# Graph attention with two residual layers on one core: written order on every engine, x kept on chip, q made on all partitions by one product

## The chip, the cores and the metric

The kernel runs on one core of a Trainium2 chip. The metric is the device time of one execution in microseconds (us). The kernel is written in Python against an engine-level language: every call names its engine (`nc.tensor` is TensorE, `nc.vector` VectorE, `nc.scalar` ScalarE, `nc.gpsimd` GpSimd, `nc.sync` the queue that issues most transfers), and a tile framework adds the semaphores. A pool with `bufs=n` gives n buffers to each tag; a tile that finds all of them in use waits until the oldest is free.

## The reference

Inputs are x (32 batches, 512 x 1024, float32), an adjacency matrix adj (512 x 512), two vectors wq and wk of 512, and biases. Only these steps are computed:

```python
# layer 0, per batch; C = 512, N = 1024
q = einsum('c,bcn->bn', wq, x)
k = einsum('c,bcn->bn', wk, x)
scores = q[:, None, :] + k[:, :, None]
scores = where(scores > 0, scores, 0.01 * scores)
att = softmax(scores, axis=-1)
agg = einsum('bcn,bmn->bcm', x, att)
x = layernorm(x + relu(einsum('oc,bcm->bom', adj, agg) + bm[None, :, None]))
# layer 1
W = adj * adj
x = layernorm(x + einsum('bnf,nm->bmf', x, W) + bias)
```

The 1024 x 1024 attention matrix is never made. Leaky ReLU splits each row of scores at q > -k, and on both sides exp(q + k) factors into a part of q and a part of k. So the kernel sorts the columns of z = adj x by q, forms running sums from both ends with the two weights, and each output column needs one row of either sum, found by counting how many q exceed -k.

## The kernel before

A batch goes through these functions. Names of tiles are those of the profile (z_ps, zbuf, sorted_z, up, zs, table, got, agg_ps, t, w, l_ps, g).

```python
xp = ctx.enter_context(tc.tile_pool(name="xp", bufs=2))
gp = ctx.enter_context(tc.tile_pool(name="gp", bufs=2))
# p2: 3 PSUM tiles of two banks, p1: 2 PSUM tiles of one bank

def scores(b):
    # ... t4 = four partial (q, k) pairs on TensorE, copied to qk4 by ScalarE
    for h in range(NH):
        nc.tensor.matmul(t2[0:2, h * H : (h + 1) * H], pick, qk4[:, h * H : (h + 1) * H], start=True, stop=True)
    nc.scalar.copy(rows, t2[0:2, :])
    for h in range(NH):        # q on all partitions
        nc.tensor.matmul(tq[:, h * H : (h + 1) * H], ones_row, rows[0:1, h * H : (h + 1) * H], start=True, stop=True)
    for j in range(NT):        # q and k as columns
        nc.tensor.transpose(tk[:, j, :], rows[:, j * P : (j + 1) * P], ident[0:2, 0:2])
    # ... qb = tq with its maximum (VectorE); eight ranks (VectorE), eight Sign counts (ScalarE)

def product(b, s):             # z = x^T adj^T, rows scattered to their ranks
    for j in range(NT):
        for c in range(CT):
            nc.tensor.matmul(t, xt[:, c, j * P : (j + 1) * P], adj_t[:, c, :], start=(c == 0), stop=(c == CT - 1))
        z = zbuf[j % ZB]       # ZB = 4
        nc.scalar.copy(z[:, 0:C], t)
        nc.gpsimd.tensor_copy(z[:, D : D + 1], s["qk"][:, j, 0:1])
        nc.gpsimd.indirect_dma_start(out=zd[:, :], ..., in_=z[:, :])

def sums(b, s):                # load sorted z, running sums up and down, carries, table
    nc.sync.dma_start(out=zs, in_=zd.rearrange("(p j) c -> p j c", j=NT))
    # ... ac: two exponents (ScalarE); 8 steps up into `up`, 8 steps down in zs (VectorE)
    # ... carries across partitions: TensorE, copied by ScalarE
    # ... carry added to `up`, written as the left half of each table row in three DMAs,
    #     then to zs, written as the right half in two

def mixed(b, s):               # one table row per output column
    for i in range(NT // G):   # G = 4
        for j in range(G):
            nc.gpsimd.indirect_dma_start(out=g[:, j, :], out_offset=None, in_=tb[:, :], ...)
        # ... weights w (VectorE), then per j: right half scaled (ScalarE), left half added (VectorE)

def layer0(b, parts):
    for o in range(CT):
        t = tp.tile([P, N], F32, tag="t", name=f"t_{b}_{o}")
        nc.sync.dma_start(out=t, in_=x[b, o * P : (o + 1) * P, :])
        # ... 8 transposes of parts into ps; t = max(ps, -bm) + t; mean, squares; then w2 = adj_2 / deviation

def layer1(b, ts, ws):
    # ... 32 products of 128 x 128 by 512 into ps; g = ps + bias; mean, squares
    for m, g in enumerate(gs):
        nc.vector.tensor_scalar(g, g, nmean[:, m : m + 1], rs[:, m : m + 1], ALU.add, ALU.mult)
        nc.sync.dma_start(out=out[b, m * P : (m + 1) * P, :], in_=g)

for i in range(B + 2):
    # load(i + 1), product(i), mixed(i - 1), scores(i + 1), layer1(i - 2), sums(i), layer0(i - 1)
```

This order is only a priority: the framework's scheduler may move an instruction ahead of another one on the same engine.

Of the kernel before, what the change touches and what calls it, by code (L numbers as in the profile page):

```python
# [26 lines left out]
BF16 = mybir.dt.bfloat16  # L27
U32 = mybir.dt.uint32
# [11 lines left out]
def adj_resnorm_kernel(  # L40
# [20 lines left out]
    xp = ctx.enter_context(tc.tile_pool(name="xp", bufs=2))  # L61
    one = ctx.enter_context(tc.tile_pool(name="one", bufs=1))
    gp = ctx.enter_context(tc.tile_pool(name="gp", bufs=2))
    tp = ctx.enter_context(tc.tile_pool(name="tp", bufs=CT + 1))
    op = ctx.enter_context(tc.tile_pool(name="op", bufs=CT))
    wp = ctx.enter_context(tc.tile_pool(name="wp", bufs=CT))
    sp = ctx.enter_context(tc.tile_pool(name="sp", bufs=2))
    dr = ctx.enter_context(tc.tile_pool(name="dr", bufs=1, space=bass.MemoryType.DRAM))
    p2 = ctx.enter_context(tc.tile_pool(name="p2", bufs=3, space=bass.MemoryType.PSUM))
    p1 = ctx.enter_context(tc.tile_pool(name="p1", bufs=2, space=bass.MemoryType.PSUM))  # L70

    def load(b):
        t = xp.tile([P, CT, N], F32, tag="x", name=f"x_{b}")
        for c in range(CT):
            nc.sync.dma_start(out=t[:, c, :], in_=x[b, c * P : (c + 1) * P, :])
        return t

    xts = {0: load(0)}


    ident = const.tile([P, P], F32, name="ident")
    make_identity(nc, ident)
    ones_row = const.tile([1, P], F32, name="ones_row")
    nc.vector.memset(ones_row, 1.0)
# [23 lines left out]
    wqk = const.tile([P, CT, 32], F32, name="wqk")  # L108
    nc.vector.memset(wqk, 0.0)
    nc.scalar.dma_start(out=wqk[:, :, 0:1], in_=wq.rearrange("(t p o) -> p t o", p=P, o=1))  # L110
    nc.scalar.dma_start(out=wqk[:, :, 1:2], in_=wk.rearrange("(t p o) -> p t o", p=P, o=1))
# [7 lines left out]
    nbm = const.tile([P, CT], F32, name="nbm")  # L119
    nc.scalar.dma_start(out=nbm, in_=bm.rearrange("(t p) -> p t", p=P))  # L120
    nc.vector.tensor_scalar(nbm, nbm, -1.0, None, ALU.mult)
    bias_b = const.tile([P, N], F32, name="bias_b")
    nc.scalar.dma_start(out=bias_b, in_=bias.partition_broadcast(P))

    adj_t = const.tile([P, CT, C], F32, name="adj_t")
    adj_2 = const.tile([P, CT, C], F32, name="adj_2")
    for r in range(CT):
        a = tp.tile([P, C], F32, tag="t", name=f"adj_{r}")
        nc.scalar.dma_start(out=a, in_=adj[r * P : (r + 1) * P, :])
        nc.vector.tensor_tensor(adj_2[:, r, :], a, a, ALU.mult)  # L130
        nc.vector.tensor_tensor(
            adj_2[:, r, r * P : (r + 1) * P], adj_2[:, r, r * P : (r + 1) * P], ident, ALU.add
        )
        t = p1.tile([P, CT, P], F32, tag="m", name=f"adj_tp_{r}")
        for c in range(CT):
            nc.tensor.transpose(t[:, c, :], a[:, c * P : (c + 1) * P], ident)
        nc.vector.tensor_copy(adj_t[:, :, r * P : (r + 1) * P], t)


    ZB = 4  # L140
    zbuf = [const.tile([P, ZR], F32, name=f"zbuf_{i}") for i in range(ZB)]
    for t in zbuf:
        nc.vector.memset(t[:, C : C + 1], 1.0)
    zero = const.tile([1, D], F32, name="zero")
# [3 lines left out]
    for t in table:  # L148
        nc.scalar.dma_start(out=t[N : N + 1, D:], in_=zero)

# [6 lines left out]
    def scores(b):  # L157
        xt = xts[b]
# [7 lines left out]
        qk4 = one.tile([P, N], F32, tag="qk4", name=f"qk4_{b}")  # L166
        for h in range(NH):
            nc.scalar.copy(qk4[:, h * H : (h + 1) * H], t4[:, h * H : (h + 1) * H])  # L168
        t2 = p2.tile([P, N], F32, tag="w", name=f"row_ps_{b}")
        for h in range(NH):  # L170
            nc.tensor.matmul(  # L171
                t2[0:2, h * H : (h + 1) * H], pick, qk4[:, h * H : (h + 1) * H],
                start=True, stop=True,
            )
        rows = one.tile([2, N], F32, tag="rows", name=f"rows_{b}")
        nc.scalar.copy(rows, t2[0:2, :])
        tq = p2.tile([P, N], F32, tag="w", name=f"q_ps_{b}")
        for h in range(NH):
            nc.tensor.matmul(
                tq[:, h * H : (h + 1) * H], ones_row, rows[0:1, h * H : (h + 1) * H],  # L180
                start=True, stop=True,
            )
        tk = p1.tile([P, NT, 2], F32, tag="m", name=f"col_ps_{b}")
        for j in range(NT):
            nc.tensor.transpose(tk[:, j, :], rows[:, j * P : (j + 1) * P], ident[0:2, 0:2])
        qb = one.tile([P, N], F32, tag="qb", name=f"qb_{b}")
        top = sp.tile([P, 1], F32, tag="top", name=f"top_{b}")
        nc.vector.tensor_scalar(qb, tq, 1.0, None, ALU.mult, ALU.max, accum_out=top)
        qk = sp.tile([P, NT, 2], F32, tag="qk", name=f"qk_{b}")
        nc.vector.tensor_copy(qk, tk)  # L190
        ntop = sp.tile([P, 2], F32, tag="ntop", name=f"ntop_{b}")
        nc.vector.tensor_scalar(ntop[:, 0:1], top, -1.0, None, ALU.mult)
        nc.vector.tensor_scalar(ntop[:, 1:2], top, -SLOPE, None, ALU.mult)

        rank = sp.tile([P, NT], F32, tag="rank", name=f"rank_{b}")
        sign = sp.tile([P, NT], F32, tag="sign", name=f"sign_{b}")
        for j in range(NT):
            junk = one.tile([P, N], BF16, tag="junk_v", name=f"junk_v_{b}_{j}")
            at = N - P - j * P
            nc.vector.scalar_tensor_tensor(  # L200
                junk, qb, qk[:, j, 0:1], tie[:, at : at + N], ALU.subtract, ALU.is_gt,
                accum_out=rank[:, j : j + 1],
            )
        for j in range(NT):
            junk = one.tile([P, N], BF16, tag="junk_s", name=f"junk_s_{b}_{j}")
            nc.scalar.activation(  # L206
                junk, qb, AF.Sign, bias=qk[:, j, 1:2], accum_out=sign[:, j : j + 1]
            )
        to = sp.tile([P, NT], U32, tag="to", name=f"to_{b}")
        nc.vector.tensor_copy(to, rank)  # L210
        of = sp.tile([P, NT], U32, tag="of", name=f"of_{b}")
        nc.vector.tensor_scalar(of, sign, 0.5, N / 2, ALU.mult, ALU.add)

        bd = sp.tile([P, 2, NT], F32, tag="bd", name=f"bd_{b}")
        nc.vector.tensor_scalar(bd[:, 0, :], qk[:, :, 1], top, 0.0, ALU.add, ALU.min)
        nc.vector.tensor_scalar(bd[:, 1, :], qk[:, :, 1], top, 0.0, ALU.add, ALU.max)
        nc.scalar.activation(bd[:, 0, :], bd[:, 0, :], AF.Exp, scale=1.0 - SLOPE)
        nc.scalar.activation(bd[:, 1, :], bd[:, 1, :], AF.Exp, scale=SLOPE - 1.0)
        return dict(qk=qk, ntop=ntop, to=to, of=of, bd=bd)

    def product(b, s):

        xt, zd = xts.pop(b), sorted_z[b % 2]
        ins = []
        for j in range(NT):
            t = p1.tile([P, C], F32, tag="m", name=f"z_ps_{b}_{j}")
            for c in range(CT):
                nc.tensor.matmul(  # L228
                    t, xt[:, c, j * P : (j + 1) * P], adj_t[:, c, :],
                    start=(c == 0), stop=(c == CT - 1),  # L230
                )
            z = zbuf[j % ZB]
            nc.scalar.copy(z[:, 0:C], t)  # L233
            nc.gpsimd.tensor_copy(z[:, D : D + 1], s["qk"][:, j, 0:1])  # L234
            ins.append(
                nc.gpsimd.indirect_dma_start(  # L236
                    out=zd[:, :], out_offset=bass.IndirectOffsetOnAxis(ap=s["to"][:, j : j + 1], axis=0),
                    in_=z[:, :], in_offset=None,
                ).ins
            )  # L240
        apart(f"ranks {b}", ins)

    def sums(b, s):

        zd, tb = sorted_z[b % 2], table[b % 2]
        zs = one.tile([P, NT, ZR], F32, tag="zs", name=f"zs_{b}")
        nc.sync.dma_start(out=zs, in_=zd.rearrange("(p j) c -> p j c", j=NT))
        ac = sp.tile([P, 2, NT], F32, tag="ac", name=f"ac_{b}")
        nc.scalar.activation(ac[:, 0, :], zs[:, :, D], AF.Exp, bias=s["ntop"][:, 0:1])
        nc.scalar.activation(ac[:, 1, :], zs[:, :, D], AF.Exp, scale=SLOPE, bias=s["ntop"][:, 1:2])  # L250
        up = one.tile([P, NT, D], F32, tag="up", name=f"up_{b}")
        nc.vector.tensor_scalar(up[:, 0, :], zs[:, 0, 0:D], ac[:, 0, 0:1], None, ALU.mult)
        for j in range(1, NT):
            nc.vector.scalar_tensor_tensor(  # L254
                up[:, j, :], zs[:, j, 0:D], ac[:, 0, j : j + 1], up[:, j - 1, :], ALU.mult, ALU.add
            )
        L = NT - 1
# [133 lines left out]
    for i in range(B + 2):  # L391
        if i + 1 < B:
            xts[i + 1] = load(i + 1)
# [41 lines left out]
```

## Time and profile before

| what | value |
|---|---|
| median of 3 runs | 3123.7 us (3109.84 to 3128.26) |
| profiled run | 3110.03 us, span 3108.3 us |
| busy: TensorE / VectorE / ScalarE / GpSimd | 2406.7 / 1710.3 / 1151.9 / 639.2 us |
| mean granted TensorE clock | 0.87 of full |
| moved by DMA | 608.14 MB, mean 196 GB/s |
| DMA queues, share of 16 engines | SyncE's 43.3%, GpSimd's 19.7% |

The page of the profile gives the busy time of each engine and the same in 40 equal slices. Its group lines name line, engine, operation, output and inputs, shape and count, then busy time and mean of one, then the idle time just before and what ended it. L228 is the product, L236 the scatter, L303 the gather, L200 the ranks, L206 the counts, L254 and L260 the sums up and down, L284, L286 and L292 the table's writes, L373 layer 1, L378 its output, L386 its normalization. "PEld" is the loading of a matmul's stationary operand, "SPq" the queue of SyncE. One float32 product of the source shows as two matmul instructions.

### The profile page before, as it was taken

The page shows a single profiled execution, that of the slowest core. Times are in us where ns is not written, and L with a number is a line of the kernel's source. Part 1 is how long each engine was busy: PE and PEld are TensorE (multiplying, and loading weights), DVE is VectorE, ACT ScalarE, POOL GpSimd, SP SyncE. Part 2 cuts the span into 40 slices and gives each one's busy share as a digit, 9 for nine tenths or more (in the row PEclk, how much of TensorE's full clock was granted, in tenths as well). Part 3 has the DMA queues.
Part 4 walks back from the last instruction along what each step waited for, and adds up shares of the span by engine and source line. Part 5 has one row for each costly group of instructions (what it writes and reads, how often), then busy time and mean ns, then how long its engine had stood idle before and what let it go on. Part 6 is the DMA issues. An engine that isn't in the chain of part 4 may idle for free.

```text
span 3108.3 us, 21737 instructions
## 1 busy us (share of the span) xinstructions
PE 2406.7 (77%) x6416; PEld 1050.7 (34%) x6416; DVE 1710.3 (55%) x3230; ACT 1151.9 (37%) x1982; POOL 639.2 (21%) x777
## 2 busy tenths in 40 slices
PE   6559877878778878778777778787777787788857
PEld 2224332333333334333333333343333343333423
DVE  4356654456645566644566445666445665445653
ACT  3134433334434344433344333344333444333422
POOL 2220222211222211222202222112222111222110
PEclk8779988989888889889898888898898988888968
DMA  5655656766566756567665577665677665685563
GB/s 190 190 152 160 222 196 192 244 164 199 202 190 220 221 177 204 201 186 230 195 177 203 184 217 238 162 204 200 192 222 206 187 200 199 188 239 177 162 203 129
DMA packets 187835, 608.14 MB, mean 196 GB/s; under 512 B 19106, under 2 KB 19106, under 8 KB 183620
## 3 DMA queue, kind: packets, MB, share of 16 engines
q1 hardware_dynamic: 128064, 403.28, 43.3%
q0 software_dynamic: 57344, 201.88, 19.7%
q10 hardware_dynamic: 2308, 1.58, 0.2%
q8 instruction: 51, 0.84, 0.1%
q14 instruction: 68, 0.56, 0.1%
HBM read 337.65 MB, written 269.03 MB: 195 GB/s over the span
## 4 chain that ended last, share of the span: by engine, by line
issue 30%; DVE 22%; PE 17%; DMA 16%; POOL 13%; ACT 2%; POOLq 0%; DVEq 0%; ACTq 0%
DMA got<-table,of 11%; DVE junk_v L200 7%; POOL got L303 6%; PE l_ps L373 6%; PE z_ps L228 5%; POOL sorted_z L236 5%; DMA sorted_z<-zbuf,to 4%; DVE g L378 3%; DVE up L254 3%; DVE got L318 3%; PE agg_ps L348 2%; PE row_ps L171 2%; POOL zbuf L234 2%; DVE zs L260 2%; ACT zbuf L233 1%
## 5 line engine op out<-in xcount | busy, mean ns | idle before, releaser
L373 PE MATMUL l_ps<-t,w 128*128 128x512 f32 x2048 | 1023.3, 663 | 247.9 <-DVE g L378 222.2
L228 PE MATMUL z_ps<-adj_t,x 128*128 128x512 f32 x2048 | 920.4, 600 | 47.4 <-ACT zbuf L233 47.4
L373 PEld LDWEIGHTS l_ps<-t,w 128*128 128x128 f32 x2048 | 432.9, 215 | 813.4 <-issue 546.6
L309 DVE TENSOR_TENSOR w<-bd,got 128x4 f32<-128x4 f32 x64 | 10.7, 167 | 1163.7 <-DMA got<-table,of 963.8
L228 PEld LDWEIGHTS z_ps<-adj_t,x 128*128 128x128 f32 x2048 | 380.1, 192 | 498.6 <-issue 418.1
L236 POOL DMA_INDIRECT sorted_z<-zbuf,to x256 | 276.7, 1081 | 1259.0 <-DVE g L386 1028.1
L233 ACT COPY zbuf<-z_ps 128x512 f32<-128x512 f32 x256 | 149.2, 583 | 859.0 <-DMA sorted_z<-zbuf,to 523.7
L200 DVE SCALAR_TENSOR_TENSOR junk_v<-qb,qk,tie 128x1024 bf16<-128x1024 f32 x256 | 327.4, 1279 | 0.4 <-DVE w L310 0.2
L317 ACT ACTIVATE got<-got,w 128x512 f32<-128x512 f32 x256 | 163.8, 711 | 428.1 <-DVE w L315 175.5
L234 POOL COPY zbuf<-qk 128x1 f32<-128x1 f32 x256 | 116.8, 478 | 998.8 <-DMA sorted_z<-zbuf,to 805.5
L206 ACT ACTIVATE junk_s<-qb,qk 128x1024 bf16<-128x1024 f32 x256 | 292.1, 1141 | 75.1 <-DVE qk L190 72.0
L171 PE MATMUL row_ps<-qk,pick 128*2 128x512 f32 x128 | 106.7, 982 | 267.5 <-ACT qk L168 267.5
L327 ACT ACTIVATE junk<-g,nmean 128x1024 bf16<-128x1024 f32 x128 | 147.0, 1149 | 364.7 <-DVE nmean L381 364.7
L303 POOL DMA_INDIRECT got<-table,of x256 | 242.8, 949 | 143.0 <-issue 69.8
L318 DVE SCALAR_TENSOR_TENSOR got<-got,w 128x512 f32<-128x512 f32 x256 | 175.3, 746 | 27.2 <-issue 15.8
L378 DVE SCALAR_TENSOR_TENSOR g<-l_ps,bias_b 128x1024 f32<-128x1024 f32 x128 | 155.9, 1218 | 35.1 <-PE l_ps L373 34.8
L254 DVE SCALAR_TENSOR_TENSOR up<-zs,ac,up 128x513 f32<-128x513 f32 x224 | 168.5, 752 | 4.4
L327 ACT ACTIVATE junk<-t,nmean 128x1024 bf16<-128x1024 f32 x128 | 146.6, 1145 | 64.1 <-DVE nmean L352 63.0
L260 DVE SCALAR_TENSOR_TENSOR zs<-zs,ac 128x513 f32<-128x513 f32 x224 | 167.4, 747 | 3.8
L348 PE MATMUL agg_ps<-ident,got 128*128 128x128 f32 x1024 | 142.8, 284 | 33.2 <-DVE g L378 32.6
L349 DVE SCALAR_TENSOR_TENSOR t<-agg_ps,nbm,t 128x1024 f32<-128x1024 f32 x128 | 161.0, 1274 | 2.7 <-PE agg_ps L348 2.7
L278 DVE TENSOR_TENSOR up<-up,carry 128x1539 f32<-128x1539 f32 (+2 forms) x96 | 148.9, 1576 | 4.2 <-ACT carry L269 1.9
(82 smaller groups left out, 1409.4 us busy)
## 6 DMA issues: line engine op xcount, KB each, us to landing
zs<-sorted_z SPq DMA_DIRECT2D x32, 2056.0 KB
table<-zs SPq DMA_DIRECT2D x64, 1026.0 KB
x<-in_x_dram SPq DMA_DIRECT2D x128, 512.0 KB
t<-in_x_dram SPq DMA_DIRECT2D x128, 512.0 KB
out_dram<-g SPq DMA_DIRECT2D x128, 512.0 KB
table<-up SPq DMA_DIRECT2D x32, 1026.0 KB
table<-up SPq DMA_DIRECT2D x32, 769.5 KB
table<-carry SPq DMA_DIRECT2D x32, 256.5 KB
```

The lines of the kernel that those rows point to most:

```text
L200: nc.vector.scalar_tensor_tensor(junk, qb, qk[:, j, 0:1], tie[:, at : at + N], ALU.subtract, ALU.is_gt, accum_out=rank[:, j : j + 1],)
L206: nc.scalar.activation(junk, qb, AF.Sign, bias=qk[:, j, 1:2], accum_out=sign[:, j : j + 1])
L228: nc.tensor.matmul(t, xt[:, c, j * P : (j + 1) * P], adj_t[:, c, :], start=(c == 0), stop=(c == CT - 1),)
L236: nc.gpsimd.indirect_dma_start(out=zd[:, :], out_offset=bass.IndirectOffsetOnAxis(ap=s["to"][:, j : j + 1], axis=0), in_=z[:, :], in_offse ...
L254: nc.vector.scalar_tensor_tensor(up[:, j, :], zs[:, j, 0:D], ac[:, 0, j : j + 1], up[:, j - 1, :], ALU.mult, ALU.add)
L260: nc.vector.scalar_tensor_tensor(zs[:, j, 0:D], zs[:, j, 0:D], ac[:, 1, j : j + 1], zs[:, j + 1, 0:D], ALU.mult, ALU.add)
L303: nc.gpsimd.indirect_dma_start(out=g[:, j, :], out_offset=None, in_=tb[:, :], in_offset=bass.IndirectOffsetOnAxis(ap=s["of"][:, i * G + j ...
L318: nc.vector.scalar_tensor_tensor(g[:, j, 0:C], g[:, j, 0:C], w[:, 0, j : j + 1], g[:, j, D : D + C], ALU.mult, ALU.add)
L327: nc.scalar.activation(junk, t, AF.Square, bias=nmean[:, i : i + 1], accum_out=var[:, i : i + 1])
L348: nc.tensor.transpose(ps[:, j * P : (j + 1) * P], parts[j][:, o * P : (o + 1) * P], ident)
L373: nc.tensor.matmul(ps[:, at], ws[n][:, m * P : (m + 1) * P], ts[n][:, at], start=(n == 0), stop=(n == CT - 1),)
L378: nc.vector.scalar_tensor_tensor(g, ps, 1.0, bias_b, ALU.mult, ALU.add, accum_out=tot[:, m : m + 1])
```

## The change

It has five parts.

1. Every engine runs its instructions as they are written (`manual_schedule`), and the main loop interleaves three batches by hand: product and sums of batch i, gather and mix of i - 1, both layers of i - 2, and the normalization of i - 3.
2. x stays on chip from its load to layer 1 (4 buffers); layer 0 writes its result over it, and the second load of x goes.
3. q comes to all partitions by one product with a 128 x 128 matrix of equal columns; k comes as columns by eight one-column products; q's columns are picked from the diagonal blocks of qb on VectorE.
4. z has eight buffers for its scatters; their q column is filled by one VectorE copy.
5. The last normalization goes from VectorE to ScalarE.

The core of the diff:

```diff
-    xp = ctx.enter_context(tc.tile_pool(name="xp", bufs=2))
+    xp = ctx.enter_context(tc.tile_pool(name="xp", bufs=4))
-    gp = ctx.enter_context(tc.tile_pool(name="gp", bufs=2))
-    tp = ctx.enter_context(tc.tile_pool(name="tp", bufs=CT + 1))
+    ctx.enter_context(tc.manual_schedule())
 # ...
+    pick_q = const.tile([P, P], F32, name="pick_q")
+    nc.vector.tensor_copy(pick_q, pick[:, 0:1].broadcast_to([P, P]))
+    zt = const.tile([P, NT, ZR], F32, name="zt")
 # ... scores
-                tq[:, h * H : (h + 1) * H], ones_row, rows[0:1, h * H : (h + 1) * H],
+                tq[:, h * H : (h + 1) * H], pick_q, s.qk4[:, h * H : (h + 1) * H],
 # ...
-            nc.tensor.transpose(tk[:, j, :], rows[:, j * P : (j + 1) * P], ident[0:2, 0:2])
+            nc.tensor.matmul(
+                tk[:, j : j + 1], s.qk4[:, j * P : (j + 1) * P], pick[:, 1:2], start=True, stop=True
+            )
 # ...
+            nc.vector.scalar_tensor_tensor(
+                junk[:, 0:P], s.qb[:, j * P : (j + 1) * P], 1.0, ident, ALU.mult, ALU.mult,
+                accum_out=s.q[:, j : j + 1],
+            )
 # ... layer 0 over x, no second load
-            nc.sync.dma_start(out=t, in_=x[b, o * P : (o + 1) * P, :])
+            t[:, o, :], ps, nbm[:, o : o + 1], t[:, o, :], ALU.max, ALU.add,
 # ... one buffer of all eight gathered rows instead of two of four
+            s.got = one.tile([P, NT, 2 * D], F32, tag="got", name=f"got_{b}")
 # ... last normalization
-            nc.vector.tensor_scalar(g, g, nmean[:, m : m + 1], rs[:, m : m + 1], ALU.add, ALU.mult)
+        nc.scalar.activation(
+            g, g, AF.Identity, bias=s.nb[:, m : m + 1], scale=s.v1[4][:, m : m + 1]
+        )
 # ... main loop
+    for i in range(B + 3):
+        new, cur, old, past = i + 1 < B, i < B, 0 <= i - 1 < B, 0 <= i - 2 < B
+        last = 0 <= i - 3 < B
+        if new:
+            load(i + 1)
+        if cur:
+            product_start(i)
+        for j in range(NT):
+            if cur:
+                product(i, j)
+                if j < 5 or not old:
+                    nc.gpsimd.memset(spare, 0.0)
+                scatter(i, j)
+            if last and j < 4:
+                if j == 0:
+                    layer1_norm(i - 3)
+                layer1_end(i - 3, j)
+            if past and j < CT:
+                layer0(i - 2, j)
+            if past and j == CT - 1:
+                layer0_end(i - 2)
+            if old and j >= 4:
+                gather(i - 1, 2 * j - 8)
+                gather(i - 1, 2 * j - 7)
+            if new:
+                if j == 3:
+                    scores_parts(i + 1)
+                if j == 4:
+                    scores_whole(i + 1)
+                    ranks(i + 1)
+                if j >= 5:
+                    counts(i + 1, 3 * j - 15, min(3 * j - 12, NT))
+        if new:
+            scores_end(i + 1)
+        if old:
+            mix_weights(i - 1)
             for j in range(NT):
+                mix(i - 1, j)
         for m in range(CT):
+            if past:
+                layer1(i - 2, m, 0)
+            if cur and m == CT - 1:
+                carry(i, 1)
+            if past:
+                layer1(i - 2, m, 1)
+                layer1_out(i - 2, m)
+            if cur:
+                if m == 0:
+                    sums_load(i)
+                    sums_up(i)
+                if m == 1:
+                    sums_down(i)
+                if m == 2:
+                    carry(i, 0)
+                    table_up(i)
+        if cur:
+            table_down(i)
```

`scores_parts` holds the products of x with wq and wk, `scores_whole` what follows up to q and k, `layer1(b, m, h)` half of an output tile, `layer1_out` its bias, mean and squares. `table_up` writes the left halves of the table's rows in pieces of four and three steps, `table_down` the right halves in two pieces of four.

## The prediction

> **What bounds the kernel now.** I read the page's busy shares and slices first, then the waits, then one period of the steady state in the stage table and in the timeline of the DMA queue.
>
> ```profile
> PE 2406.7 (77%) x6416; PEld 1050.7 (34%) x6416; DVE 1710.3 (55%) x3230; ACT 1151.9 (37%) x1982; POOL 639.2 (21%) x777
> ...
> DMA  5655656766566756567665577665677665685563
> ```
>
> No engine is full: TensorE leads with 77%, and the 16 DMA engines are 50 to 70% busy in every slice. So the bound is a chain that passes from one to the other. The waits say which (engine, line, what it waited for: us in total, times, longest):
>
> ```profile
> POOL sorted_z L236 <- DVE g L386: 1028.1, 27, 40.0
> DVE w L309 <- DMA got<-table,of: 963.8, 57, 42.4
> POOL zbuf L234 <- DMA sorted_z<-zbuf,to: 805.5, 123, 12.9
> ...
> ACT zbuf L233 <- DMA sorted_z<-zbuf,to: 523.7, 80, 14.0
> ```
>
> VectorE loses 964 us, 30 per batch, until gathered rows arrive; ScalarE cannot empty the product's PSUM because the four scatter buffers are still in flight. One period (1505.10 us to 1599.2 us) cut into stages, with busy time and count for PE, PEld, DVE, ACT, POOL, then granted clock, DMA share and GB/s:
>
> ```profile
> 1505.00:1529.00 24.00, 24.00 (x59) 10.61 (x57) 13.22 (x16) 7.84 (x15) 5.10 (x5) 1.00 0.99 254
> 1529.00:1545.00 16.00, 7.20 (x25) 1.56 (x25) 0.00 (x0) 3.15 (x5) 6.33 (x9) 0.79 0.62 193
> 1545.00:1588.00 43.00, 34.28 (x75) 15.12 (x74) 28.64 (x64) 20.44 (x35) 8.12 (x11) 0.80 0.45 169
> 1588.00:1599.00 11.00, 9.10 (x46) 5.21 (x45) 10.93 (x22) 4.54 (x7) 0.12 (x1) 1.00 0.59 222
> ```
>
> In the first stage the DMA engines are full (0.99); in the second VectorE does nothing for 16 us. What fills the queues is in the timeline (start, us, queue, line):
>
> ```profile
> 1506.78 0.33 SPq L273 DMA_DIRECT2D table<-carry  x1
> 1508.88 2.57 SPq L284 DMA_DIRECT2D table<-up  x2
> 1511.80 0.24 SPq L286 DMA_DIRECT2D table<-up  x1
> 1514.13 2.56 SPq L292 DMA_DIRECT2D table<-zs  x2
> 1529.38 1.43 SPq L75 DMA_DIRECT2D x<-in_x_dram  x3
> ```
>
> The table's 4.2 MB leave here. By the packet records of the trace (2,052 bytes is half a table row) the last one ends a mean 25.2 us after the first L284 issue (21.6 to 31.2 over 32 batches), with 0.7 MB of scatters in between: about 200 GB/s, slow beside x. The x packets issued at 1529.38 begin only when the table's end, at 1532. I count periods from one first L284 issue to the next: 90.6 us for batch 0, 3004.8 for batch 31, so (3004.8 - 90.6)/31 = 94.0 us, and 90.6 + 103.5 = 194 us stand outside.
>
> [...] x begins behind the table writes of the same queue, while a scatter from the other queue takes its share (issued 1511.26, its buffer free at 1521.92, against 1504.69 to 1509.28 before the table writes). [...] a product instruction is 0.43 us apart in the first stage and 0.86 us at 1546, after the gap. [...]
>
> **The change, part by part.** Removed per batch: four x reloads, 2.1 MB of 19 MB, 5.8 us of the 61 us for which the DMA engines are busy (63% of 94 and some); the row products, 3.3 us of busy time (L171 has 106.7 us in all, over 32); the 1.0 us row copy on ScalarE (L176); four normalizations on VectorE, 95.2/32 = 3.0 us; eight single-column POOL copies, 3.7 us. Added: eight one-column products against whole 128-column weights, 8 x 0.28 = 2.2 us (the pair L267), less the small transposes, 0.8; eight diagonal picks on VectorE[...]; four normalizations on ScalarE at about 1.15 us (as L327), 4.6 us; a few POOL memsets.
>
> TensorE's own floor, warm: product 64 x 0.43 = 27.5, layer 1 the same, 32 transposes at 0.134 = 4.3, scores 1.9 + 1.7 + 2.2, carries 2.5: 67.6 us a batch. VectorE stays at 53, ScalarE rises from 36 to 41. By busy time alone a period of 68 us would do, 194 + 31 x 68 = 2300 us. I don't expect it, because order is now fixed and one loop runs through every engine.
>
> That loop I add up from the landing of x(i+1), called L. PE's program has the scores' first product at j=3, so everything behind it waits for L.
>
> L to scatter and gather: scores 1.9 plus product j=4 3.4 plus some 2.5 for a cold clock = 7.8; q and k products 3.9, to 11.8; product j=5 3.4 and its copy 0.9, to 16.1. Now ScalarE has three Sign counts (1.22 each) before each copy: copy 6 ends at 20.4, copy 7 at 24.7. Scatter 7 issues by 26.4 and gathers 6 and 7 by 29.0 (1.27 each). From the last gather's issue to its rows I take 6 us (the last batch shows 3037.2 to 3042.57): 35. Sorted z arrives earlier: 26.4 + 4.5 for the scatter + 8 for the load = 39, beside the next step.
>
> Mix, sums, first table write: weights 1.2; mix 0.7 + 8 x 0.69 + 0.2 = 6.4; first layer-1 output 1.3; its square on ScalarE and the two exponents 2.1, to 46; sums up 0.48 + 7 x 0.78 = 5.9; output 1.4; sums down 5.9; output 1.4; first carry addition 2.3: 63 us from L to the first table write.
>
> First table write back to L: 25 us for the table. It no longer has the end of an output store ahead of it (about 1 us less) but four scatters in its time instead of about three (1 us more). Then x in the same ring, since the new load is written after the table's writes: 2.1 MB at 5.8 us[...]: 33 us. During it TensorE does four products and the transposes, 18 us, and then stands.
>
> Sum: 63 + 33 = **96 us**, against 94.0. With the same ends (the first table write cannot come before the first ranks; the tail is a gather, a mix, layer 0 and one layer 1 as before) that is 194 + 31 x 96 = 3170 us.
>
> **Rivals.** First, x lands in time. If the table drains in some 14 us, then x is there about 20 us after the first write, when PE gets to j=3, and nothing stands. The loop is then PE's 37.5 us to product 7, then copy, gather, mix and sums, to the second carry, and the last half product: I get 78 us, so 194 + 31 x 78 = 2610 us. For it: the first microsecond or three of table packets are quick (about 90 ns each, later 150 to 190), the DMA has less to carry, and whoever put the scores at j=3 expected x by then. Against it: all 32 batches took over 21 us, the first one too, which had no output store and no reload beside it.
>
> Second, TensorE becomes the bound, near 68 us and 2300 us in all. It needs the sums to hide behind layer 1 altogether, but carry 0 sits after three quarters of it and the 63 us chain has only 21 us of product work that could lie under sums and mix. I give it a few per cent.
>
> Third, in-order waits that I have not added: copies of the product behind Sign counts or behind a normalization that waits for VectorE, POOL's gathers ahead of a scatter. Before, the scheduler let ready work pass; now one late item holds its whole engine. Each 3 us here is 93 us of the total: 100 us a period gives 3290.
>
> **Range and chances.** I give the 96 us loop and its neighbours (92 to 100) about 68%, the early x about 27%, the rest to the extremes. The loop's terms are summed with every hand-over, so I lean to its lower side: 3080 us, a period of 93. Eight in ten: 2680 to 3240. Faster by over 2% means under 3061, a period of 92.5: nearly all of the early x and a fifth of the loop, 0.43. Within 2% (to 3186, period 96.5) 0.34. Slower 0.23.
>
> **What would show it.** For the loop: in the stage table a DMA share of 1.0 for 25 to 33 us from the first table write; TensorE idle some 10 us before qk_ps with a wait for "DMA x"; the got wait of VectorE much shorter than 964 us in all; a second TensorE gap of 5 to 8 us at the first carry. DMA megabytes must fall by 67 to about 541; PE busy by little. Wrong would be: no wait of qk_ps for x; table writes done in 15 us; or a period under 85 us, which would mean that the 63 us overlaps with the 33 somewhere.

## The result and the profile after

The changed kernel takes 3030.27 us (median of 4 runs, 3026.72 to 3045.41) against 3122.07 for the kernel before: a ratio of 0.972, with a 95% interval of 0.9674 to 0.9765. That is inside the forecast range and faster than the forecast 3080; the gain is 2.8%, where 1.4% was forecast. The periods tell the same: from one first table write to the next, 90.9 us ((2920.4 - 102.0)/31) instead of 94.0, and 213 us instead of 194 outside them.

The page after, with the lines that answer to those shown of before, and its total of moved bytes:

```profile
PE 2398.7 (79%) x6544; PEld 1088.3 (36%) x6544; DVE 1763.1 (58%) x3483; ACT 1264.9 (42%) x2110; POOL 549.6 (18%) x684
...
DMA  2566557565567565567565566564675655675661
...
DMA packets 169403, 541.02 MB, mean 178 GB/s; under 512 B 17059, under 2 KB 17059, under 8 KB 165189
```

Still no engine is full and the DMA share still swings between 5 and 7 tenths, though 67 MB fewer are moved. The chain was rebuilt, not removed. The waits after (engine, tile and line, what it waited for: us in total, times, longest):

```profile
PE carry_ps L306 <- DVE up L285: 263.9, 32, 24.4
...
DVE w L357 <- DMA got<-table,of: 232.6, 32, 19.1
...
PE qk_ps L176 <- DMA x<-in_x_dram: 205.3, 41, 11.5
```

VectorE's wait for gathered rows fell from 963.8 to 232.6 us. In its place TensorE waits for x, 205.3 us or 6.4 a batch. The kernel before has no such line. One period (1465.37 to 1557.40 us) cut by stages; columns as in the table of before: busy time and count of PE, PEld, DVE, ACT, POOL, then clock, DMA share, GB/s.

```profile
1465.80:1497.60 31.80, 25.76 (x79) 11.32 (x81) 15.57 (x27) 14.86 (x21) 4.25 (x8) 0.88 0.97 266
1497.60:1523.40 25.80, 25.80 (x78) 12.01 (x71) 14.83 (x41) 14.30 (x25) 12.43 (x12) 0.98 0.53 179
1523.40:1538.50 15.10, 14.60 (x35) 6.11 (x33) 7.56 (x17) 6.53 (x14) 0.43 (x2) 1.00 0.60 232
1538.50:1557.40 18.90, 9.72 (x19) 4.46 (x20) 16.38 (x24) 3.88 (x10) 0.00 (x0) 0.82 0.04 14
```

For 32 us the DMA engines are full (0.97) with the table and x. In the last stage they carry next to nothing (0.04), TensorE works half of the time, and VectorE makes the sums. So transfers and sums stand one behind the other. The timeline of SyncE's queue at the end of this period (start, us, queue, line, count) shows the link:

```profile
1557.40 2.04 SPq L333 DMA_DIRECT2D table<-up  x2
1559.79 0.78 SPq L336 DMA_DIRECT2D table<-up  x1
1563.51 2.57 SPq L342 DMA_DIRECT2D table<-zs  x2
1566.16 2.82 SPq L77 DMA_DIRECT2D x<-in_x_dram  x4
```

x goes out behind the table's 4.2 MB in the same queue. What it holds up is in TensorE's timeline; the bracket is the idle time just before and what ended it:

```profile
1492.76 7.21 PE L176 MATMUL qk_ps<-x,wqk 128*32 128x512 f32 x16 [6.04 <-DMA x<-in_x_dram]
1499.89 3.70 PE L254 MATMUL z_ps<-adj_t,x 128*128 128x512 f32 x8
1503.43 1.88 PE L188 MATMUL q_ps<-qk,pick_q 128*128 128x512 f32 x4
1505.15 1.84 PE L194 MATMUL k_ps<-pick,qk 128*128 128x1 f32 x16
...
1544.71 2.05 PE L306 MATMUL carry_ps<-up,before 128*128 128x512 f32 x2 [6.71 <-DVE up L285]
```

TensorE stands 6 us, then takes 7.21 us for scores that take 1.92 us at 53.11 us of the same trace, where x is there in time, because they trickle in with the four pieces of x, for which TensorE waits another 1.47, 1.56 and 1.09 us. The loading of the stationary operand shows when the last piece is there:

```profile
1497.39 0.20 PEld L176 LDWEIGHTS qk_ps<-x,wqk 128*32 128x32 f32 x7 [1.09 <-DMA x<-in_x_dram]
```

That is 32.0 us after the first table write. The second gap of TensorE is the wait for the sums (6.71 us).

### The profile page after: what moved, and what is told of

The parts are those of the page before. It is cut to its first block, busy times and chain, and to the rows that moved or that the text cites. A ratio compares the mean times of both kernels' runs of the same rounds, so it can differ in the third digit from the quotient of the medians.

```text
span 3031.6 us, 21745 instructions
## 1 busy us (share of the span) xinstructions
PE 2398.7 (79%) x6544; PEld 1088.3 (36%) x6544; DVE 1763.1 (58%) x3483; ACT 1264.9 (42%) x2110; POOL 549.6 (18%) x684
## 2 busy tenths in 40 slices
DMA packets 169403, 541.02 MB, mean 178 GB/s; under 512 B 17059, under 2 KB 17059, under 8 KB 165189
## 3 DMA queue, kind: packets, MB, share of 16 engines
q1 hardware_dynamic: 109632, 336.16, 38.5%
## 5 line engine op out<-in xcount | busy, mean ns | idle before, releaser
L415 PE MATMUL l_ps<-x,w 128*128 128x512 f32 x2048 | 971.3, 633 | 18.9 <-DVE w L406 15.4
L263 POOL DMA_INDIRECT sorted_z<-zt,to x256 | 283.7, 1108 | 2265.3 <-issue 1305.5
L415 PEld LDWEIGHTS l_ps<-x,w 128*128 128x128 f32 x2048 | 415.3, 206 | 522.8 <-issue 517.5
L176 PE MATMUL qk_ps<-x,wqk 128*32 128x512 f32 x512 | 197.1, 819 | 214.6 <-DMA x<-in_x_dram 205.3
L220 DVE SCALAR_TENSOR_TENSOR junk_v<-qb,q,tie 128x1024 uint8<-128x1024 f32 x256 | 328.7, 1284 | 8.0
L258 ACT COPY zt<-z_ps 128x512 f32<-128x512 f32 x256 | 148.2, 579 | 365.3 <-PE z_ps L254 365.3
L231 ACT ACTIVATE junk_s<-qb,k 128x1024 bf16<-128x1024 f32 x256 | 294.0, 1148 | 10.4 <-DVE k L201 5.2
L395 DVE SCALAR_TENSOR_TENSOR x<-agg_ps,nbm,x 128x1024 f32<-128x1024 f32 x128 | 164.1, 1282 | 203.4 <-PE agg_ps L394 203.4
L315 DVE TENSOR_TENSOR up<-up,carry 128x2052 f32<-128x2052 f32 (+2 forms) x96 | 149.0, 1580 | 58.0 <-ACT carry L310 57.0
L440 ACT ACTIVATE g<-g,nb,rs 128x1024 f32<-128x1024 f32 x128 | 158.4, 1240 | 19.9 <-DVE nb L435 19.9
```

The lines of the kernel that those rows point to most:

```text
L176: nc.tensor.matmul(t4[32 * c : 32 * c + 32, h * H : (h + 1) * H], wqk[:, c, :], xt[:, c, h * H : (h + 1) * H], start=True, stop=True,)
L220: nc.vector.scalar_tensor_tensor(junk, s.qb, s.q[:, j : j + 1], tie[:, at : at + N], ALU.subtract, ALU.is_gt, accum_out=s.rank[:, j : j + 1],)
L231: nc.scalar.activation(junk, s.qb, AF.Sign, bias=s.k[:, j : j + 1], accum_out=s.sign[:, j : j + 1])
L263: nc.gpsimd.indirect_dma_start(out=sorted_z[b % 2][:, :], out_offset=bass.IndirectOffsetOnAxis(ap=s.to[:, j : j + 1], axis=0), in_=zt[:, j ...
L395: nc.vector.scalar_tensor_tensor(t[:, o, :], ps, nbm[:, o : o + 1], t[:, o, :], ALU.max, ALU.add, accum_out=s.v0[0][:, o : o + 1],)
L415: nc.tensor.matmul(s.ps[:, at], s.w2[:, n, m * P : (m + 1) * P], t[:, n, at], start=(n == 0), stop=(n == CT - 1),)
```

## The experiments

The theory: one loop sets the period: table writes, x behind them in the same ring, scores, counts, gather, mix, sums, table writes. Its rivals were that x lands in time anyhow, that TensorE is the bound, and that in-order waits elsewhere make up the period. Ratios are to the kernel before on the same chip, with 95% intervals. Unless said otherwise that kernel took 3118 to 3120 us there (3122 beside the changed kernel), so times of those runs can be laid beside the changed kernel's 3030.

**load_mid: x ahead of the right half of the table.**

```diff
-        if new:
-            load(i + 1)
+        if i == 0:
+            load(1)
 # ... after table_up(i), before table_down(i)
+        if i + 2 < B:
+            load(i + 2)
```

> x(i+2) is issued between the left and the right halves of the table, not behind both. Theory A (the loop: table writes, then x in the same ring, then TensorE's scores, counts, gather, mix, sums, table): x lands some 17 us after the first table write, when TensorE comes to it, and the wait of qk_ps for x goes from 205 us to under 30; the table's end moves 6 us back to about 31 us, and the gathers become what is waited for: 31 + 14 for eleven descriptors + 5 + 7 + 3 + 14 + 2.3 = 77 us a period, 213 + 31 x 77 = 2600 us (2530 to 2700). Theory B (the DMA engines' total work sets the time, and the gain came from the 67 MB less): the same bytes, so 3030 within 1%. Theory C (in-order holds in mix and sums set the time): within 30 us of 3030.

Measured: 3045.42 us, 0.9768 (0.9719 to 0.9816). No gain. TensorE's waits for x fell to 20.7 us, but ScalarE's waits have a new line:

```profile
ACT qk L182 <- DMA out_dram<-g: 280.0, 28, 13.1
```

ScalarE cannot copy qk_ps into `qk4`, because the tile `qk4` shares its tag with the output tiles `g` and takes a buffer over from one of them. That buffer's store to `out_dram` now stands where x stood, behind the right half of the table in the same ring:

```profile
1469.80 2.31 SPq L77 DMA_DIRECT2D x<-in_x_dram  x4
1473.46 2.58 SPq L342 DMA_DIRECT2D table<-zs  x2
1479.24 9.01 SPq L443 DMA_DIRECT2D out_dram<-g  x4
```

So the ring has two doors to the scores, x itself and the buffer of `qk4`. Opening one only showed the other.

**load_mid_qk: both doors open.** As load_mid, and `qk4` in a buffer that no store empties:

```diff
-        s.qk4 = op.tile([P, N], F32, tag="g", name=f"qk4_{b}")
+        s.qk4 = one.tile([P, N], F32, tag="qb", name=f"qk4_{b}")
```

> load_mid again, and the tile that takes the scores from PSUM (qk4) shares the buffer of qb in place of one of the four output tiles g. In load_mid its copy waited 280 us in all for an output store, which stands in the same ring behind the table. Theory A, with this second door (the scores wait for the ring once through x and once through the output tile that qk4 takes over): with both open the gathers, which need the whole table, are the bound; period 77 to 79 us, 213 + 31 x 78 = 2630 us (2560 to 2720). Theory B (x ahead of half the table only moves the table's end back, and the same bytes take the same time): 3030 within 1%. Theory C (mix and sums in written order): the same.

Measured: 2759.37 us, 0.8855 (0.8832 to 0.8878), a period of 81.9 us. Same instructions and bytes, 271 us less than the changed kernel. The wait of ScalarE for `out_dram` is gone, and TensorE's for x is 20.1 us in all. From first table write to the copy of the scores the mean over 25 periods falls from 33.9 to 24.3 us. The direction and the mechanism are borne out; the size fell short of the expected 2630, 3.9 us a period. Of these 2.9 us are the first gather: it starts 33.9 us after the first table write, not at 31.

**scores_late: no transfer is moved; the scores come three products later.**

```diff
-                if j == 3:
+                if j == 6:
                     scores_parts(i + 1)
-                if j == 4:
+                if j == 7:
 # ...
-                if j >= 5:
-                    counts(i + 1, 3 * j - 15, min(3 * j - 12, NT))
+                    counts(i + 1, 0, NT)
```

> No transfer is moved; TensorE's scores go from j=3 and 4 to j=6 and 7, the counts behind the last product's copy. Theory A: products 4 to 6 run while x is on its way, the stall before qk_ps shrinks from 10 us to 2 to 4, scatter 7 issues at about 36 us after TensorE's start of a period in place of 54, the ranks of VectorE then hold the mix to about 51: period about 81, 213 + 31 x 81 = 2720 us (2640 to 2820). Theory B: the same bytes, 3030 within 1%. Theory C: within 1% too, since mix and sums stay as they were, or slower by the ranks in front of the mix (3100).

Measured: 2810.3 us, 0.9011 (0.8989 to 0.9034), a period of 83.5. The scores are asked for later, yet the kernel is 220 us faster: products and scatters that need nothing of x(i+1) no longer stand behind it. From first table write to the first gather it is 27.0 instead of 39.6 us. TensorE's wait at this place all but goes:

```profile
1471.12 1.90 PE L176 MATMUL qk_ps<-x,wqk 128*32 128x512 f32 x10 [0.53 <-DMA x<-in_x_dram]
```

**again_ahead and again_behind: how much is a byte in the ring worth?** 2.1 MB of x are stored from the chip to unused memory, as a stand-in for the second load of x that the change took out; once just ahead of the load of x, once just behind it.

```diff
+    def again(b):
+        for c in range(CT):
+            nc.sync.dma_start(out=spill[b % 2][c * P : (c + 1) * P, :], in_=xts[b][:, c, :])
 # ...
         if new:
+            if i > 0:
+                again(i)        # again_ahead; again_behind has it after the next line
             load(i + 1)
```

> 2.1 MB more per batch (x written to a spare place in DRAM, its size and packets those of a reload), put in the ring just ahead of the load of x. Theory A: L, the landing of x, comes 5.8 us later in each period, so 31 x 5.8 = 180 us more: 3210 us (3150 to 3260). Theory B: 5.8 us more DMA work a batch, but only as far as the engines are the bound; the same as in again_behind. Theory C: no change, 3030 within 1%.

> The same 2.1 MB more per batch, put in the ring just behind the load of x. Theory A: nobody waits for what follows there (the output stores have until the sorted z is loaded), so 0 to 1 us a period: 3030 to 3060 us. Theory B: as again_ahead, both slower by the same amount. Theory C: 3030 within 1%.

Measured: ahead 3144.11 us, 1.0084 (1.0057 to 1.011), 114 us or 3.5 us a period over the changed kernel; behind 3080.66 us, 0.9879 (0.9853 to 0.9905), 50 us over it. The same bytes cost over twice as much ahead of x as behind it. So the place in the ring counts, though less than the 5.8 us a period that I had expected. Ahead of x they move its last piece from 31.5 to 35.1 us after the first table write (means over 30 periods), and the rest of the period stays at 60 us. Behind x they leave it where it was (31.4), but they are not free either: they delay the output stores and so `qk4`, and the wait of ScalarE for `out_dram` is 360.8 us there. Why the bytes ahead of x cost it 3.6 and not 5.8 us no run shows.

**pitch: shorter table writes, same order.** The two halves of a table row start 528 floats apart instead of 513, so every written half starts at a multiple of 64 bytes. Still 2,052 bytes are written per half; the gather reads 4,224 bytes instead of 4,104.

```diff
+    W = 528
-    table = [dr.tile([N + 1, 2 * D], F32, name=f"table_{i}") for i in range(2)]
+    table = [dr.tile([N + 1, 2 * W], F32, name=f"table_{i}") for i in range(2)]
 # ...
-            ...(out=rows[:, lo:hi, D:], in_=s.zs[:, lo:hi, 0:D])
+            ...(out=rows[:, lo:hi, W : W + D], in_=s.zs[:, lo:hi, 0:D])
 # ... readers of the right half likewise; the pads are zeroed once; small tiles moved to make room
```

> The changed kernel with half rows of the table 528 floats apart in place of 513, so that each half starts at a multiple of 64 bytes; still 2,052 bytes are written per half row, gathers read 4,224 bytes. If the odd starts make the table's writes slow, 25 us fall to about 15 and, by theory A, the period by as much as the scores let it, 8 us: 213 + 31 x 83 = 2790 us. If the rate is that of writes of this size whatever their start: 3030 to 3060 us (the gathers 3% longer, some 10 us more before the first batch).

Measured: 2755.44 us, 0.8832 (0.8818 to 0.8847), a period of 82.7. The queue lines (packets, MB, share of 16 engines), the changed kernel first, then pitch:

```profile
q1 hardware_dynamic: 109632, 336.16, 38.5%
```

```profile
q1 hardware_dynamic: 109632, 336.16, 32.9%
```

The same packets and bytes take 38.5% of 3031.6 us, 1167 us, and 32.9% of 2773.4 us, 912 us. In the packet records a 2,052-byte packet has a mean of 154 ns in the changed kernel and 93 ns here, and the table's last packet ends a mean 14.9 us after the first table write instead of 23.7. These 8.8 us come off the period almost whole (8.2). The starts of the half rows and their distance changed together; which of the two counts, and what it does inside the memory, no run shows.

**no_manual: the changed kernel without its fixed order.**

```diff
-    ctx.enter_context(tc.manual_schedule())
```

> The changed kernel without its written order: the framework's scheduler may move ready work ahead again, all else as it is. In the order that it makes, x(i+1) still stands behind the table on its queue. Theory A: the wait for x stays, but products can run during it; 2850 to 3030 us. Theory C (written order holds engines): clearly faster than 3030, by over 3%. If written order is what brought the gain: 3030 to 3150 us.

Measured: 2670.96 us, 0.8554 (0.8537 to 0.8572), a period of 79.8. So the fixed order, with all else the same, turns 0.855 into 0.972. It costs 359 us; the rest of the change earns 14.5% under the scheduler. The direction is that of theory C, in-order waits, and the range of theory A is missed. The queue's timeline shows one thing that the scheduler did:

```profile
1362.81 2.71 SPq L332 DMA_DIRECT2D table<-up  x2
1366.86 2.41 SPq L76 DMA_DIRECT2D x<-in_x_dram  x4
1376.31 2.58 SPq L341 DMA_DIRECT2D table<-zs  x2
```

From the third batch on it put three or four of x's four loads between the halves of the table, as load_mid does by hand. This I had not expected. ScalarE's copies of the scores do not wait for `out_dram` there either. So the 359 us are the price of this fixed order with its place of x in the ring. load_mid_qk, still in a written order, gets 271 of them back; what makes up the rest was not isolated.

**best: a written order without the loop.** It is load_mid_qk, and sums up and down follow each other, carries and the left half of the table come before the last three outputs of layer 1, and two of those outputs come after the table:

```diff
+        if past:
+            layer1(i - 2, 0, 0)
+            layer1(i - 2, 0, 1)
+            layer1_out(i - 2, 0)
+        if cur:                     # after the mix
+            sums_load(i)
+            sums_up(i)
+            sums_down(i)
 # ... outputs 1 to 3 of layer 1: products here, carries between them
+        if cur:
+            table_up(i)
+        if i + 2 < B:
+            load(i + 2)
 # ... layer1_out 1, table_down(i), layer1_out 2 and 3
```

> load_mid_qk with another order behind the counts: the first output of layer 1 is taken before the mix, sums up and sums down follow each other without an output between, the two carries and the first table writes come before outputs 1 to 3. Theory A: some 4 us less between the mix and the first table write and 1.5 us less in front of the exponents: period 72 to 75 us, 213 + 31 x 74 = 2510 us (2430 to 2600). If instead TensorE is held by the later outputs (PSUM tiles not free), period 78 and no gain over load_mid_qk.

Measured: 2557.35 us, 0.8204 (0.8186 to 0.8222), a period of 75.2 us. The engines of one such period:

```profile
1381.30:1455.60 74.30, 69.86 (x210) 33.24 (x209) 54.78 (x109) 39.78 (x68) 17.11 (x21) 0.98 0.74 227
```

TensorE is busy for 69.86 of 74.30 us. Only now is it close to being the bound, near the floor of 67.6 us that the prediction added up. A fixed order is thus not slow in itself; this one is 4% under the scheduler's 2671 us.

**Which parts earn the 14.5%?** zb8 is the kernel before with eight scatter buffers instead of four. nm_zb4 is no_manual with four scatter buffers and the q column copied per scatter on GpSimd, as before. nm_again is no_manual with the 2.1 MB stand-in ahead of x. These ran on another chip, where the kernel before took 3234.84 us, and beside them best_pitch, which joins best and pitch.

```diff
-    ZB = 4
+    ZB = 8          # zb8
```

```diff
-        nc.scalar.copy(zt[:, j, 0:C], t)
+        nc.scalar.copy(zbuf[j % 4][:, 0:C], t)                              # nm_zb4
+        nc.gpsimd.tensor_copy(zbuf[j % 4][:, D : D + 1], s.q[:, j : j + 1])
```

> The kernel before with eight scatter buffers in place of four and nothing else. The run without written order took 2671 us, so the other parts of the change are worth 450 us under the scheduler. Theory D (four scatter buffers held TensorE's product while scatters stood behind the table's writes: ACT zbuf waited 524 us for them, and the scores come behind the product): most of the 450 us comes from here, 2750 to 2900 us. Theory E (the second load of x, 2.1 MB just ahead of the output store and the table in the ring, and two x buffers): under 60 us from here, 3060 to 3120 us.

> The changed kernel without written order, and with four scatter buffers filled as before (q column by one GpSimd copy each). Theory D: loses most of what that kernel gained, 2950 to 3100 us. Theory E: 2670 to 2730 us.

> The changed kernel without written order, with 2.1 MB more per batch on SyncE's ring (x written to a spare place in DRAM, in the size and packets of a reload). Theory E: loses 150 to 300 us, 2820 to 2970. Theory D: the scheduler's order leaves room, 2670 to 2760 us.

> best with the half rows at multiples of 64 bytes as in pitch. In best the first gather starts 33.9 us after the first table write and the weights follow at 53.8. With the table done 9 us earlier the gathers start at about 25 and the next bound is TensorE, 67.6 us of work and some gaps: period 69 to 72 us, 213 + 31 x 70.5 = 2400 us (2340 to 2460). If the gathers are not what best waits for: 2540 to 2570 us.

Measured: zb8 3087.48 us, 0.9542 (0.9521 to 0.9564); nm_zb4 2942.24, 0.9095 (0.9071 to 0.9119); nm_again 2808.05, 0.8681 (0.8661 to 0.8702); best_pitch 2528.45, 0.7816 (0.7798 to 0.7834). Since the kernel before is slower there, these ratios don't compare with those of the first chips. Even so, zb8 lies between the two theories (D says 0.88 to 0.93 of the kernel before, E 0.98 to 1), nm_again in neither range, and best_pitch misses its 2400 us by 128. For a comparison on one chip, no_manual, nm_zb4, best and best_pitch ran together on one more, where the kernel before took 3113.3 us; these runs end in one_chip.

> The changed kernel without written order again, on one chip with the next: 0.855 of the kernel before, as on the first chip (0.85 to 0.865); if that chip's slower transfers matter, nearer to 0.88.

> The same with four scatter buffers. Theory D (the buffers are a main part of the gain): 1.05 to 1.07 times nm_one_chip, as 0.9095 against 0.8554 on two chips. If that was the chip: under 1.03 times.

> best on one chip with best_pitch: 0.82 of the kernel before (0.81 to 0.83).

> best with aligned half rows. If the gathers are what best waits for, 4 to 6% under best_one_chip. best_pitch on another chip showed a period of 75.1 us with the first gather only 4 us earlier than in best and the weights not earlier at all (53.5 against 53.8), so I now expect 0 to 2% under best_one_chip: TensorE, busy 89%, and the scores' own way are the bound.

Measured: nm_one_chip 2651.13 us, 0.8511 (0.849 to 0.8532); nm_zb4_one_chip 2872.44, 0.923 (0.9202 to 0.9259). Four scatter buffers instead of eight, with the copy per scatter, cost 221 us, 8.3%, more than the 5 to 7% of theory D. The wait they bring back, in nm_zb4:

```profile
POOL zbuf L258 <- DMA sorted_z<-zbuf,to: 611.7, 132, 12.1
```

So the eight buffers, with the one copy that serves them, are a main part of what the change earns. In the kernel before, the buffers alone are worth 4.6%: there the wait for scatters on ScalarE goes (5.7 us, from 523.7), but VectorE's wait for gathered rows is 1147.1 us in all, where it was 963.8.

best_one_chip took 2558.66 us, 0.8217 (0.8195 to 0.8239), and best_pitch_one_chip 2527.43, 0.8117 (0.8097 to 0.8137). Once x is off the loop, the shorter table writes, worth 275 us in the changed kernel, are worth 31: the first gather starts 30.2 instead of 34.1 us after the first table write, but the weights of the mix only 0.8 us earlier, at 53.5. best_pitch is the fastest version, 18.8% under the kernel before.

## Why the prediction was right or wrong

**What failed is a size: the 96 us of the loop.** The path was right, but both terms of the sum were too long. For the 63 us from the landing of x to the first table write the runs show 59.9, and for the 33 us from there to the landing 31.5, together 91.4 (means over the 30 periods that load an x). With the ends, which are longer than forecast, the change gained 92 us, where 44 were forecast.

**The loop: right.** The forecast signs are all there: a DMA share of 0.97 for 32 us, TensorE's wait for x ahead of qk_ps (6 us and 5 more in the trickle, with 10 forecast), the wait for gathered rows down to a quarter, a 6.71 us gap at the first carry, 541.02 MB. load_mid_qk, scores_late and pitch each cut one link and each shortened the period, by 9.0, 7.4 and 8.2 us. The table below divides the period at TensorE's start on the last piece of x (us, means over 30 periods); the experiments move the part that they were aimed at:

| kernel | first table write to last piece | last piece to next table write |
|---|---|---|
| changed kernel | 31.5 | 59.9 |
| again_ahead | 35.1 | 60.0 |
| again_behind | 31.4 | 61.3 |
| pitch | 23.3 | 59.6 |
| scores_late | 32.4 | 51.4 |
| load_mid | 21.6 | 70.3 |
| load_mid_qk | 21.6 | 60.6 |

**"33 us" from first table write to x: nearly right.** 31.5 us, and 32.0 in the period shown. The excess is in the writes of the table. Counted on the same clock as the issues, the packet records of the kernel before have their end a mean 23.6 us after the first L284 issue (19.9 to 29.5), not 25.2, and x begins at 1530, not 1532; in the changed kernel it is 23.7. This step rests on x starting behind the table's writes of its queue. The runs show it: in the changed kernel the first packet of x starts a mean 10.3 us after the first issue of x (5.6 to 16.3 over 30 batches), 3.9 us before the last packet of the table ends; bytes ahead of x in its ring made it 3.6 us later (35.1 instead of 31.5), the same bytes behind it did not (31.4). What the 33 us held beyond 25.2 for the table and 5.8 for x was shown by no trace.

**"63 us" from x to the first table write: mis-sized.** By the forecast's own marks, in us from the landing of x, in the period shown:

| mark | forecast | measured |
|---|---|---|
| scores and product 4 | 7.8 | 6.2 |
| q and k | 11.8 | 9.6 |
| copy 5 | 16.1 | 13.8 |
| last gather issued | 29.0 | 26.4 |
| its rows | 35 | 31.1 |
| start of sums up | 46 | 41.2 |
| first table write | 63 | 60.0 |

The largest error is the first mark. I had added 2.5 us for a cold clock behind the landing, my estimate, as product instructions were 0.86 us apart instead of 0.43 after the gap in the kernel before. Here too the granted clock was 0.50 after the gap of 6.04 us. But most of the slow time lay under the earlier pieces of x (columns as above; the granted clock is the third number from the end):

```profile
1492.70:1497.40 4.70, 4.64 (x7) 0.56 (x7) 0.00 (x0) 0.00 (x0) 0.00 (x0) 0.50 0.86 350
1497.40:1500.00 2.60, 2.60 (x12) 0.76 (x11) 0.00 (x0) 0.00 (x0) 0.00 (x0) 0.74 0.52 211
1500.00:1503.60 3.60, 3.60 (x9) 1.69 (x10) 0.00 (x0) 1.07 (x2) 0.00 (x0) 1.00 0.16 65
```

The gather took 4.75 us instead of 6. A pick of q's columns on VectorE took 0.29 us (L205), one every 0.33 us. The sums gave 1.8 us back, since VectorE's first carry addition waited for ScalarE's copy of the carry:

```profile
1555.07 4.69 DVE L315 TENSOR_TENSOR up<-up,carry 128x2052 f32<-128x2052 f32 x3 [1.90 <-ACT carry L310]
```

**The ends: wrong the other way.** 213 us instead of 194. The first table write comes at 102.0 instead of 90.6 us; TensorE's timeline at the start shows most of that:

```profile
44.04 9.13 PE L254 MATMUL z_ps<-adj_t,x 128*128 128x512 f32 x16 [7.81 <-ACT zt L258]
```

The first batch's copies of the product stand behind its eight counts and two exponents on ScalarE, and TensorE waits for them 7.81 us. "The first table write cannot come before the first ranks" left this out. The other 7.7 us are in the tail.

**The lean to 3080: in part luck.** The worked sum of 96 us said 3170, slower than before. The true terms give 213 + 31 x 90.9 = 3031. I took off 3 us a period because the terms were summed with every hand-over. It was the right direction and too little: 5.1 us were needed, 3.1 from the 63, 1.5 from the 33, and 0.5 because the last period, 75.8 us, has no x to wait for. That 3080 lies within 50 us of the result is because two errors offset each other: periods 2.1 us too long make 65 us, the ends were 19 us too short.

**Rival 1, x in time: didn't occur,** but load_mid_qk makes it occur. Its forecast period of 78 us was 3.9 too short.

**Rival 2, TensorE as the bound:** not in the changed kernel; nearly in best.

**Rival 3, in-order waits:** I took it for an addition to the loop, "100 us a period". In no_manual the fixed order is worth 11.1 us of a period. The scheduler lets x pass half of the table, so part of that may be the loop itself. The forecast also missed the second door: the tile `qk4` that waits for an output store. In the changed kernel a single wait of 11.3 us showed it; it took 280 us in all once x came early.

**Still open.** How the rest of the 14.5% divides between q by one product, the kept x and the moved normalization: none of them was run alone. nm_again against no_manual is a comparison across chips and doesn't settle the reload. The change of `qk4` without the earlier load wasn't tried.

## What to carry to other kernels

In this kernel's written order, a load that stands behind slow writes in the same queue (23.7 us for a table) made a whole engine wait (TensorE, 205.3 us in all), and with it all that is written behind the consumer. Put the load ahead of the writes (load_mid_qk, 271 us less) or the consumer later (scores_late, 220 us less), and then look for the second door: a tile that takes over a buffer which a store in the same queue still has to empty (280.0 us of waits in load_mid). Before fixing an order by hand, run the same parts under the scheduler; here that separates a gain of 14.5% from a loss that ate most of it.

## What the runs showed of the hardware that I had not expected

Writes of 2,052 bytes took a mean of 153 ns per packet in the kernel before and 154 ns in the changed kernel, where row halves lie 513 floats apart, and 93 ns in pitch, where they lie 528 apart and start at multiples of 64 bytes, with the same bytes. The medians, 86, 85 and 87 ns, hardly differ, so it is a part of the packets that is slower: 21% take over 150 ns in the changed kernel, 3% in pitch.

One chip ran the kernel before in 3234.84 us and another in 3113.3, while best_pitch took 2528.45 and 2527.43 on the two. The difference goes with these packets: in nm_zb4, rows 513 floats apart, they took a mean of 174.5 ns on the slower chip and 155.6 on the other; in best_pitch, 528 apart, 90.4 and 90.5. Why the chips differ no run shows.
